# Exps of two attention layers turned in 32x32 blocks by VectorE, and their product in 16 or 8 blocks of TensorE's array

## The chip, the cores and the metric

The kernel runs on one core of a Trainium2 chip. A core has five engines, each of which works through its own instructions in the order in which they were put there: TensorE (PE in the profile, with its weight loads as PEld) multiplies matrices and writes to PSUM alone; VectorE (DVE), ScalarE (ACT) and GpSimd (POOL) work element by element; SyncE (SP) issues the DMAs. They wait for one another through semaphores. SBUF and PSUM have 128 partitions[...]. The metric is the device time of one execution in microseconds (us); lower is better. The kernel before takes 5228.07 us, the median of three runs (5227.61 to 5230.24).

## The reference

Four residual layers run over 32 independent graphs of 512 nodes with 256 features. Each layer norms its input, applies a ReLU, runs a graph attention under the graph's adjacency matrix, and adds the result to its input. Layers 0 and 3 are the ones that matter here; both are attention by dot products. Cut to that:

```python
# layer 0: H = 8 heads of HD = 32, queries = keys = values
qkv = layer_norm(x, gamma1, beta1).reshape(b_, n_, H, HD).transpose(0, 2, 1, 3)
scores = jnp.einsum('bhqd,bhkd->bhqk', qkv, qkv) * scale
masked = jnp.where(adj_matrix[:, None, :, :] > 0, scores, -jnp.inf)
attn = jax.nn.softmax(masked, axis=-1)
out = jnp.einsum('bhqk,bhkd->bhqd', attn, qkv)
x = x + out.transpose(0, 2, 1, 3).reshape(b_, n_, d_)
y = layer_norm(x, gamma2, beta2)
return x + jax.nn.gelu(y @ W1 + b1, approximate=False) @ W2 + b2

# layer 3: HEADS = 4 of D_K = 64, with projections q, k, v
scores = jnp.einsum('bnhd,bmhd->bhnm', q, k) * scale
attn = jax.nn.softmax(jnp.where(mask, scores, min_val), axis=-1)
out = jnp.einsum('bhnm,bmhd->bnhd', attn, v).reshape(B, N, OUT_DIM)
return jax.nn.relu(out @ Wo + bo)
```

Layers 1 and 2 are graph attentions whose logits are a sum of a term of the query and a term of the key (4 heads of 64). They are not changed. All is float32.

## The kernel before

**Tiling.** One graph ("batch" b) is held as 4 chunks of 128 rows (`NC = 4`, `P = 128`, `N = 512`, `D = 256`). `batch` (from L1726) strings the layers of one graph together: `layer0`, `gat_layer` twice, `layer3`.

**Order.** The program does not run in the order in which it is written. Every piece of work is an `Op` with an engine (or two that could do it), a planned cost in us, the tiles that it reads and writes, and the buffers that it needs. `Plan.schedule` plays all of them through with these planned costs and writes each engine's instructions down in the order in which they would start; up to `FLIGHT = 4` graphs are in flight, in `CHAINS = 3` chains. Which op goes first among those that could start is set by `key`, in which the constants `PACE`, `RAMP`, `SWITCH`, `URGENCY` and `FINE` enter. So the order is fixed at build time; on the chip an engine waits when what it needs is late.

**Attention of layers 0 and 3** (`attend`, `unit`). Heads go in groups of `G = P // dh`: four heads of 32 in layer 0, two of 64 in layer 3, two groups in each layer. For each half of the queries (two chunks of 128), each group and each query chunk:
- `dots` (L1078): scores of the G heads, each head in its own rows of the array (K = dh), 512 keys at once, into PSUM tiles `pss` of two banks (two buffers of those);
- for each head a `unit`: `masked` on DVE (L1125) scales the scores, adds the mask and takes the row's smallest value `low`, into SBUF tile `e`; `exps` on ACT (L1137) takes the exponential and its row sum; `turn` on PE (L1143) transposes the 128x512 exps in four transposes of 128x128 into PSUM bank `pst`; `evacuate` (L963) copies that bank to `eT` in SBUF, on DVE or ACT, whichever the plan picks.

After the two query chunks of a half, `product` (L1099) multiplies the values with `eT`: for each of the four key chunks and each head one matmul of 128 keys x dh values against 256 queries, each head in its own columns of the array, summed in bank `pso`. Then `finish`: layer 0 copies `pso` to `oT`, turns it back and divides by the row sums (`divide`, L1165 to L1182), and GpSimd adds it to `h` (L1502, L1503). Layer 3 spreads the reciprocals of the sums (L1649), turns them (L1656), multiplies them into `pso` (L1671), and projects (L1686 to L1693).

In float32 a matmul of the program that is no transpose stands as two matmul instructions in the trace, each with its own weight load; a transpose stands as one.

**Buffers.** Big tiles of 8 KiB per partition come from `exp_tile` (six buffers, tag "E"): two for a half of a group in layer 0, one in layer 3, two for a pair of heads in layers 1 and 2, two for the MLP's `gT`. The exps `e` of units have eight buffers of 2 KiB (`E_UNITS`). PSUM holds two tiles of two banks (`two`) and four of one bank (`one`).

**SP's queue.** SP issues the loads of the adjacency rows (L1715, two buffers, freed when POOL has made the mask of them at L1720), of x, and the stores.

```python
def turn(e):
    for c in ALL:
        nc.tensor.transpose(ps.t[:, c, :], ex.t[:, bass.ts(c, P)], ident)
```

## Time and profile before

The profiled execution took 5227.27 us, of which 5225.5 us are the span of the program's instructions; the granted clock of TensorE was 0.991 of full speed.

| what | value |
| --- | --- |
| median of three runs | 5228.07 us |
| profiled execution, its span | 5227.27 us, 5225.5 us |
| PE busy, share of the span | 97% |
| DVE, ACT, POOL busy | 61%, 70%, 52% |
| HBM traffic | 87.97 MB read, 16.78 MB written |

In a line of a group of instructions stand the line of the code, the engine, the operation, the tiles written and read with their shapes, the count after x, then busy time in us and the mean of one in ns, then the idle time of the engine before them and what ended it. Matmuls overlap in the array, so the mean of one matmul is longer than the step from one to the next. A busy time counts overlapping instructions once.

### The profile page before, as it was taken

To read this page: it belongs to the slowest core of one execution; us is meant where nothing else is said; L and a number is where in the kernel's file an instruction comes from. 1 tells how busy PE (TensorE), PEld (TensorE's weight loads), DVE (VectorE), ACT (ScalarE), POOL (GpSimd) and SP (SyncE) were. 2 spreads that over 40 slices of the span, in tenths; PEclk is the share of its full clock that TensorE was granted. 3 is DMA by queue.
4 is the path that set the end of the run, shared out by engine and by line. 5 is a ranking of instruction groups with operands and counts; after the bars stand their busy time and mean duration, and the time that the engine had idled before them with its cause. 6 is when DMAs were issued, how large, how long until landed. Compare 5 with 4: busy or idle time off the path is not lost.

```text
span 5225.5 us, 86599 instructions
## 1 busy us (share of the span) xinstructions
PE 5085.6 (97%) x30972; PEld 2810.8 (54%) x30972; DVE 3163.1 (61%) x9219; ACT 3668.6 (70%) x7053; POOL 2709.7 (52%) x3988
## 2 busy tenths in 40 slices
PE   6989999999999999999999999999999999999998
PEld 4544555555555555555555555555555555555554
DVE  5545666666565666565666666665656665666653
ACT  6747777777677777677776667776777766677755
POOL 6445544565544655445655445654446554456442
PEclk9989999999999999999999999999999999999999
DMA  2000000000000000000000000000000000000000
GB/s 84 1 9 25 20 10 21 25 25 25 17 11 23 25 25 25 11 15 25 25 25 19 11 21 25 25 25 15 13 23 25 25 25 15 11 25 25 13 13 13
DMA packets 78692, 110.31 MB, mean 21 GB/s; under 512 B 9523, under 2 KB 45238, under 8 KB 78262
## 3 DMA queue, kind: packets, MB, share of 16 engines
q1 hardware_dynamic: 70656, 100.68, 6.4%
q8 instruction: 246, 4.03, 0.3%
q10 hardware_dynamic: 7606, 4.08, 0.3%
q14 instruction: 184, 1.51, 0.1%
HBM read 87.97 MB, written 16.78 MB: 20 GB/s over the span
## 4 chain that ended last, share of the span: by engine, by line
PE 76%; POOL 13%; DVE 5%; ACT 3%; issue 2%; DMA 0%; ACTq 0%; POOLq 0%; SPq 0%; DVEq 0%
PE pst L1143 12%; PE pss L1078 9%; PE psg L1549 8%; PE psf L1528 8%; PE pso L1099 8%; POOL esum L1371 6%; PE psv L1574 4%; PE pso L1385 4%; PE psu L1441 3%; POOL mask L1720 2%; PE psk L1597 2%; PE psv L1625 2%; DVE junk L1260 2%; PE psq L1597 2%; PE psu L1433 2%
## 5 line engine op out<-in xcount | busy, mean ns | idle before, releaser
L1137 ACT ACTIVATE e<-e,low 128x512 f32<-128x512 f32 x1536 | 1102.5, 724 | 143.8 <-DVE low L1125 136.5
L1125 DVE CUSTOM_DVE_ANT_0 e<-pss,mask 128x512 f32<-128x512 f32 x1536 | 985.3, 682 | 253.3 <-PE pss L1078 212.8
L1143 PE MATMUL pst<-ident,e 128*128 128x128 f32 x6144 | 854.1, 278 | 29.9 <-ACT eT L963 20.2
L1143 PEld LDWEIGHTS pst<-ident,e 128*128 128x128 f32 x6144 | 673.0, 141 | 370.2 <-ACT e L1137 193.3
L1260 DVE CUSTOM_DVE_ANT_0 junk<-psd,mask 128x512 bf16<-128x512 f32 x1024 | 702.5, 686 | 124.3 <-PE psd L1248 93.8
L1371 POOL TENSOR_TENSOR esum<-esum,e 128x1024 f32<-128x1024 f32 x256 | 602.2, 2359 | 51.6 <-ACT e L1467 42.2
L1446 ACT ACTIVATE psu<-psu 128x1024 f32<-128x1024 f32 x512 | 509.1, 1011 | 164.7 <-PE psu L1441 164.0
L963 ACT COPY eT<-pst 128x512 f32<-128x512 f32 x954 | 520.7, 590 | 113.6 <-PE pst L1143 110.7
L1467 ACT ACTIVATE e<-psu 128x1024 f32<-128x1024 f32 x512 | 513.9, 1025 | 34.7 <-PE psu L1450 32.4
L1720 POOL TENSOR_SCALAR mask<-adj_mask 128x512 bf16<-128x512 int32 x256 | 494.2, 1931 | 53.8 <-DVE low L1125 19.1
L983 POOL TENSOR_TENSOR mw_h<-st_h 128x4 f32<-128x4 f32 x128 | 26.1, 204 | 935.4 <-DVE st_h L974 934.1
L1385 PE MATMUL pso<-e,hT 128*64 128x512 f32 x2048 | 474.8, 606 | 0.0
L1528 PE MATMUL psf<-yT,w_L_gnn_W 128*128 128x512 f32 x1024 | 457.0, 596 | 0.8 <-ACT gT L1539 0.8
L1549 PE MATMUL psg<-w_L_gnn_W,gT 128*128 128x256 f32 x2048 | 448.3, 379 | 0.4 <-ACT gT L1539 0.4
L963 DVE COPY eT<-pst 128x512 f32<-128x512 f32 x582 | 386.1, 685 | 83.2 <-PE pst L1143 73.2
L1549 PEld LDWEIGHTS psg<-w_L_gnn_W,gT 128*128 128x128 f32 x2048 | 386.4, 190 | 53.5 <-ACT gT L1539 1.2
L1371 POOL TENSOR_TENSOR esum<-e 128x1024 f32<-128x1024 f32 x128 | 301.1, 2352 | 171.6 <-ACT e L1467 160.5
L1502 POOL TENSOR_TENSOR od<-od,b_L_gnn_gamma 128x256 f32<-128x256 f32 x128 | 93.4, 730 | 519.9 <-DVE od L1182 519.7
L1008 ACT ACTIVATE h<-x,mv_h 128x256 f32<-128x256 f32 x512 | 272.2, 594 | 74.8 <-POOL mv_h L994 41.8
L1441 PE MATMUL psu<-maskT,ident 128*128 128x512 bf16 x1024 | 316.2, 391 | 0.0
L1539 ACT ACTIVATE gT<-psf,c_L_gnn_b 128x512 f32<-128x512 f32 x256 | 175.3, 689 | 196.4 <-PE psf L1528 195.9
L1528 PEld LDWEIGHTS psf<-yT,w_L_gnn_W 128*128 128x128 f32 x1024 | 188.0, 190 | 227.9 <-issue 204.5
(192 smaller groups left out, 8355.7 us busy)
## 6 DMA issues: line engine op xcount, KB each, us to landing
adj_mask<-in_adj SPq DMA_DIRECT2D x256, 256.0 KB, 2.6
x<-in_x SPq DMA_DIRECT2D x32, 512.0 KB, 3.9
out<-x SPq DMA_DIRECT2D x32, 512.0 KB, 3.2
w_L_gnn_W<-in_L_gnn_W ACTq DMA_DIRECT2D x2, 1024.0 KB, 6.6
w_L_gnn_W<-in_L_gnn_W ACTq DMA_DIRECT2D x1, 256.0 KB, 7.2
w_L_gnn_W_proj<-in_L_gnn_W_proj ACTq DMA_DIRECT2D x1, 256.0 KB, 7.4
w_L_gnn_Wo<-in_L_gnn_Wo ACTq DMA_DIRECT2D x1, 256.0 KB, 7.7
w_L_gnn_Wq<-in_L_gnn_Wq ACTq DMA_DIRECT2D x1, 256.0 KB, 7.1
```

Of the source, the lines that this page charges most:

```text
L963: lambda e: (nc.scalar.copy if e == "ACT" else nc.vector.tensor_copy)(dst(), view(src.t)),
L1125: nc.vector.tensor_tensor_reduce(out=ex.t, in0=src.t[:, j, :], in1=mask.t[:, q, :], scale=-scale, scalar=FLT_MAX, op0=ALU.add, op1=ALU.min ...
L1137: nc.scalar.activation(ex.t, ex.t, AF.Exp, bias=low.t, scale=-1.0, accum_out=total.t[:, q, h : h + 1])
L1143: nc.tensor.transpose(ps.t[:, c, :], ex.t[:, bass.ts(c, P)], ident)
L1260: nc.vector.tensor_tensor_reduce(out=junk.t, in0=dB.t, in1=mask.t[:, q, :], scale=1.0, scalar=-FLT_MAX, op0=ALU.add, op1=ALU.max, accum_ou ...
L1371: nc.gpsimd.tensor_tensor(esum.t, left, es[c // 2].t[:, c % 2, :, :], ALU.add)
L1385: nc.tensor.matmul(o.t[bass.ts(j, GD), :], v.t[:, c, bass.ts(2 * p + j, GD)], es[c // 2].t[:, c % 2, j, :], start=(c == 0), stop=(c == NC ...
L1446: nc.scalar.activation(ps.t, ps.t, AF.Prelu, alpha=SLOPE)
L1467: lambda e: nc.scalar.activation(dst.t[:, c % 2, :, :], ps.t, AF.Exp),
L1528: nc.tensor.matmul(ps.t, w1[:, d, bass.ts(f, P)], yT.t[:, d, :], start=(d == 0), stop=(d == DC - 1),)
L1549: nc.tensor.matmul(ps.t, gT[f // (FC // 2)].t[:, f % (FC // 2), bass.ts(c, P)], w2[:, f, :], start=(f == 0), stop=(f == FC - 1),)
L1720: lambda e, at=at, c=c: nc.gpsimd.tensor_scalar(mask.t[:, c, :], at.t, 0, -BIG, op, ALU.mult),
```

## The change

`unit` no longer turns the exps on PE, and nothing evacuates them. After `exps`, VectorE turns them in place in SBUF: `nc.vector.transpose` turns each 32x32 block of the 128x512 tile, but leaves the blocks where they are. So partition 32r + i, column 32k + b holds query 32r + b and key 32k + i of that chunk.

`product` therefore takes blocks of 32 keys. The array is used in pieces of 32 rows (32 keys; r, the block row of the queries) by dh columns (head j): 4 x 4 = 16 pieces in layer 0, 4 x 2 = 8 in layer 3. For each of 16 blocks k of keys, each r and each head one matmul: 32 keys x dh values against 128 queries (4 chunks of 32), summed over k in a PSUM bank of its own for each r. All four query chunks of a group go into one product, so there are two products for a layer of a graph in place of four.

Block row r needs the values of all keys on its partitions 32r to 32r + 31. `spread` makes this copy `vr` from the values in SBUF by 16 DMAs from SP for each group. The PSUM banks' columns come out in the order r, chunk, b, and `by_blocks` puts them back when they are copied or multiplied, in three parts (`parts_of`): two banks at once, then one and one.

A group takes G tiles of "E" for the exps of all chunks (`eT`) and one for `vr`, from eight buffers in place of six; the small tiles `e` are gone. Layer 3's reciprocals are spread and turned for the whole group ahead of the product (`prepare`). The plan's constants are set anew (of `URGENCY` and `FINE` nothing is shown).

```diff
-PACE = 24.3
-RAMP = 466.5
+PACE = 0.0
+RAMP = 393.0
-SWITCH = 150.8
-SKEW = {"DVE": 0.07, "ACT": 0.0}
-E_UNITS = 8
+SWITCH = 315.4
+SKEW = {"DVE": 0.12, "ACT": 0.0}
...
     def exp_tile(shape, name, b):
-        return Buf(att, shape, F32, "E", 6, name)
+        return Buf(att, shape, F32, "E", 8, name)
...
+        for g in range(H // G):
+            eT = [exp_tile([P, NC, N], f"eT_{name}_{g}_{j}", b) for j in range(G)]
+            vr = exp_tile([P, N // BL, P], f"vr_{name}_{g}", b)
+
+            def spread(e, g=g, vr=vr):
+                for r in range(P // BL):
+                    for m in range(P // BL):
+                        nc.sync.dma_start(
+                            vr.t[bass.ts(r, BL), m : N // BL : P // BL, :],
+                            v.t[bass.ts(m, BL), :, bass.ts(g, P)],
+                        )
+
+            plan.op(("SP", 9.0), spread, b, r=vkeys, w=[vr[0]], alloc=[vr, *eT])
+            for q in ALL:
...
+                plan.op(
+                    ("PE", 1.04), dots, b, r=qkeys(g) + kkeys(g),
+                    w=[t[i] for t in tiles for i in range(2)], alloc=[*tiles, vr, *eT],
+                )
+                for i in range(G):
+                    unit(eT[i], tiles[i // 2], i % 2, q, g * G + i, scale, mask, total, first, name, b)
+                    first = []
+            oT = result_tile(f"oT_{name}_{g}")
+            ready = prepare(g, oT, total)
+            o = [two(f"pso_{name}_{g}"), *(one(f"pso_{name}_{g}_{r}", [P, P]) for r in (2, 3))]
+
+            def product(e, g=g, eT=eT, vr=vr, o=o):
+                banks = [o[0].t[:, 0, 0:P], o[0].t[:, 1, 0:P], o[1].t, o[2].t]
+                for k in range(N // BL):
+                    for r in range(P // BL):
                         for j in range(G):
                             nc.tensor.matmul(
-                                o.t[bass.ts(j, dh), :],
-                                v.t[:, c, bass.ts(g * G + j, dh)],
-                                eT[j // 2].t[:, j % 2, c, :],
-                                start=(c == 0),
-                                stop=(c == NC - 1),
+                                banks[r][bass.ts(j, dh), :],
+                                vr.t[bass.ts(r, BL), k, bass.ts(j, dh)],
+                                eT[j].t[bass.ts(r, BL), :, bass.ts(k, BL)],
+                                start=(k == 0),
+                                stop=(k == N // BL - 1),
                             )
...
+            plan.op(
+                ("PE", 4.2), product, b, r=[vr[0], *ready, *(t[q] for t in eT for q in ALL)],
+                w=[t[0] for t in o], alloc=[*o, oT],
+            )
+            finish(g, o, oT, total)
...
         plan.op(
-            ("PE", 0.5), turn, b, r=[ex[0]], w=[ps[0]],
-            alloc=[ps, dst],
-        )
-        evacuate(
-            lambda: dst.t[:, j, :, bass.ts(qs, P)], [dst[j, qs]], ps, nm, b, N
+            ("DVE", 0.63), lambda e: nc.vector.transpose(ex.t[:, q, :], ex.t[:, q, :]), b,
+            w=[ex[q]],
         )
...
+        if isinstance(o, list):
+            for t, rs, view in parts_of(o):
+                cols = (rs.stop - rs.start) * P
+                plan.op(
+                    {"DVE": 0.07 + cols / 960, "ACT": 0.07 + cols / 1220},
+                    lambda e, rs=rs, view=view: (
+                        nc.scalar.copy if e == "ACT" else nc.vector.tensor_copy
+                    )(by_blocks(oT.t)[:, rs], view()),
+                    b, r=[t[0]], w=[oT[rs.start]],
+                )
```

## The prediction

> **What bounds the kernel now.** I read the page's busy line and chain first, then who waits for whom, then the groups by shape, then the timeline of one product, then DMA.
>
> ```profile
> PE 5085.6 (97%) x30972; PEld 2810.8 (54%) x30972; DVE 3163.1 (61%) x9219; ACT 3668.6 (70%) x7053; POOL 2709.7 (52%) x3988
> PE 76%; POOL 13%; DVE 5%; ACT 3%; issue 2%; DMA 0%; ACTq 0%; POOLq 0%; SPq 0%; DVEq 0%
> ```
>
> TensorE is the bound, all along the span: it waits for others for about 140 us in all. The waits list has its two largest here, the time in which matmuls (PE) and weight loads (PEld) sat idle for another engine; the second is mostly covered by matmuls that still run:
>
> ```profile
> PE pst L1143 <- ACT eT L963: 20.2, 31, 1.8
> PEld pst L1143 <- ACT e L1137: 193.3, 318, 1.6
> ```
>
> So what leaves PE's queue leaves the span, until another engine is late. The groups by shape that the change removes or multiplies:
>
> ```profile
> L1143 PE MATMUL pst<-ident,e 128*128 128x128 f32 x6144 | 854.1, 278 | 29.9 <-ACT eT L963 20.2 <-ACT e L1137 6.9 <-DVE qT L1608 0.6
> L1099 PE MATMUL pso<-eT,n 128*32 128x256 f32 x4096 | 249.7, 383 | 3.4 <-ACT eT L963 3.3
> L1099 PE MATMUL pso<-eT,hT 128*64 128x256 f32 x2048 | 249.3, 385 | 0.1
> ...
> L1125 DVE CUSTOM_DVE_ANT_0 e<-pss,mask 128x512 f32<-128x512 f32 x1536 | 985.3, 682 | 253.3 <-PE pss L1078 212.8 <-PE pst L1143 31.0 <-ACT e L1137 8.0
> L963 DVE COPY eT<-pst 128x512 f32<-128x512 f32 x582 | 386.1, 685 | 83.2 <-PE pst L1143 73.2
> L1125 DVE DVE_READ_ACCUMULATOR2_ANT low<- 128x1 f32 x1536 | 126.5, 82 | 0.0
> ...
> L963 ACT COPY eT<-pst 128x512 f32<-128x512 f32 x954 | 520.7, 590 | 113.6 <-PE pst L1143 110.7
> ```
>
> A product of layer 0 in the timeline (start and length in us): 32 matmuls of 256 columns in 1.93 us, although one takes 0.38.
>
> ```profile
> 4944.15 1.93 PE L1099 MATMUL pso<-eT,n 128*32 128x256 f32 x32
> ```
>
> In the trace's single starts it begins at 0, 6, 13 and 20 ns, then at 241, 246, 253, 260, and so on each 216 ns: four column pieces at a time, a next piece started 6.5 ns after the last, its weight load included. 216 ns for 256 columns are 0.84 ns a column. The two matmuls of one product stand next to each other in the instructions, yet the first of all four pieces start before any second: the queue looks ahead over at least 14 instructions.
>
> [...]
>
> **PE, part by part.**
> - Removed: 6144 transposes. Back to back one takes 109 ns (12 in 1.31 us), 670 us in all; with the drains around them the starts give 128 ns each, 786 us (the row's 854 us count the tails of the last ones too).
> - Removed: 128 + 128 products. From their first start to the next operation's start, 242 + 241 = 482 us.
> - Added: 64 products in layer 0 of 16 x 4 x 4 = 256 matmuls of the program, 512 instructions with 512 weight loads, and 64 in layer 3 with half as many. If all pieces run at once, each of 32 steps takes 128 columns x 0.84 = 108 ns: 3.5 us, with filling and drain 3.7 us for either layer, 128 x 3.7 = 474 us. In a step 16 starts x 6.5 ns = 104 ns just fit.
> - Sum: -786 - 482 + 474 = -794 us. The dots don't change.
>
> The unknown is the step with 16 pieces. Bounds: 6.8 ns a pair of load and matmul (above), or 27 ns (110 ns / 4) if no more than the four pieces shown ever run together. I take 6.8[...]. The instructions must also be fetched: the page's q8 moved 4.03 MB in 246 packets, 16 KB for 128 pairs, at about 1 us each (0.3% of 16 x 5225 us, over 246), which is 7.8 ns a pair: a product fetched no faster than that would take 4.0 us, within the range below.
>
> **DVE.** A block transpose of 128x512: [...]the nearest row, the copy of the same size, has 0.685. I take 0.70, 1536 x 0.70 = +1075 us. Low end 0.43 (the one SBUF copy of that size in float32, L875)[...]. Copies removed: -386. The list of instructions of the changed kernel also moves evacuations from DVE to ACT (hT, oT, qT, 245 us with their rows' means) and adds some: DVE comes to 3163 - 386 + 1075 - 227 = 3625 us.
>
> **ACT.** -521 for eT, +171 for what comes over from DVE, +128 for table loads (179 in place of 79, at 1283 ns): 3668 to about 3446 us. POOL's residuals halve in number and double in width: 2 x 0.73 against 1.27, -24 us.
>
> **SP and DMA.** 128 spreads x 16 = 2048 DMAs of 64 KB, each 128 rows of 512 B.
>
> ```profile
> q1 hardware_dynamic: 70656, 100.68, 6.4%
> q8 instruction: 246, 4.03, 0.3%
> q10 hardware_dynamic: 7606, 4.08, 0.3%
> ...
> SPq L1715 <- POOL mask L1720: 4347.0, 202, 202.6
> ```
>
> The first three are packets, MB and share of 16 engines; q10's packets, 536 B on average, took 33 ns, q1's of 1425 B took 76. So a spread takes 2048 x 33 / 16 = 4.2 us, at most 9.7, and SP issues it in 16 x 0.33 (one issue in the timeline) = 5.3 us. The cover is the group's units on DVE, (0.682 + 0.082 + 0.70) = 1.46 us each: 23 us in layer 0, 11.7 us in layer 3, where it is thin. Behind a spread in SP's queue stand the adjacency loads, which feed masks of later graphs. In front of it may stand a load that waits for POOL; the last line above shows that SP waits so nearly always, and a spread caught behind it would hold its product. I cost it at nothing, 2 us x 128 = 256 us at worst.
>
> **What is late next.** A group's units now need 1.46 us of DVE each where PE needs (297 + 280) / 1536 for the dots (rows of L1078) + 474 / 1536 = 0.68 us: attention alone is DVE-bound, and PE must fill in with other graphs. DVE in all would be 3625 of some 4500 us, 81% in place of 61%. The order is frozen from planned costs: 0.63 + 0.63 on DVE for a unit, against 1.46 measured or estimated, 0.2 us more. On 1536 units that is 307 us; before, DVE's idle 39% absorbed such errors. I let half through, +155 us. A layer 0 group holds five of eight E buffers, where two halves held two each of six; two groups of layer 0 can't overlap. That goes into the same 155.
>
> 5225.5 - 794 + 155 = 4586 us, and 1.8 us outside the span (5227.27 - 5225.5) make 4588. The median, 5228.07, lies 0.8 us above the profiled execution: 4589.
>
> **The rivals.**
> - *Part of it comes back* (17%): DVE becomes the bound in the attention stretches, the transposes cost 1 us or more, the E buffers keep graphs from overlapping, or the spreads come late. For: DVE at 81% with an order made for less. Against: PE, at 5085 - 794 = 4290 us, keeps 3240 us of other work to put beside these 1050. Time: DVE's 3625 us at 75% of the span, 4830 us; with transposes of 1 us, 3625 + 461 = 4086 us at 80%, 5110.
> - *The array or its queue doesn't run more than four pieces at once* (18%): the slower side. 64 x 512 + 64 x 256 = 49152 pairs decide: -786 - 482 is made up at 1268 us / 49152 = 25.8 ns a pair. At 27.5 ns the products take 1352 us: 5228 + 84 = about 5310 before any DVE stall; if only two run together (55 ns), 6660. For: nothing in the trace shows more than four pieces, or more than 14 instructions of look-ahead; no 3 us of it hold over 45 matmuls. Against: the evenness of 6.5 ns[...].
> - *Nothing to see* (3%): the two cancel, near 5230.
>
> **How the numbers follow.** The forecast, 62%, has its own range, 4400 to 4850: from -794 with no stall (4434) less a DVE transpose at the low end, to the full 307 us with half of the spreads late. To hold eight in ten the range takes in the first rival too, and ends where the second begins: 4360 to 5240. A change under 0.2% (10 us) could not be told from none. Faster: 62 + 17 - 1 = 78%; within 0.2%: 3%; slower: 19%.
>
> **What would show it.** Right: no pst at L1143's place, DVE transposes at 0.65 to 0.75 us, 512 matmuls of a product in 3.5 to 4.2 us, PE busy near 4300 us and still over 90%, DVE near 3600. Wrong: products over 7 us or in steps of four starts (second rival), PE idle before products, released by DVE's eT (first rival) or by the vr DMA (spreads).

## The result: slower by 18.6%, and the profile after

The changed kernel takes 6202.28 us, median of 4 runs (6191.45 to 6214.1), against 5227.84 us (4 runs, 5225.81 to 5230.24) for the kernel before, measured beside it: 1.1864 times as long, 95% interval 1.1841 to 1.1887. The forecast was 4589 us with a range of 4360 to 5240; the change is slower, and by far more than the slower rival priced for its likelier case (5310).

The page of the changed kernel, first its busy times and its chain of waits, then the granted clock of TensorE in 40 slices (tenths of full speed) and the instruction fetches:

```profile
PE 5351.7 (86%) x67706; PEld 2883.8 (46%) x67836; DVE 3550.6 (57%) x9669; ACT 3479.0 (56%) x6511; POOL 2687.0 (43%) x3860
PEclk7777888888888888888888888888888889888897
q8 instruction: 531, 8.70, 0.6%
PE 63%; ACT 15%; DVE 10%; issue 7%; POOL 2%; SPq 2%; DMA 1%; ACTq 0%; DVEq 0%; POOLq 0%
```

PE fell from 97% to 86% of the span, and other engines took its share of the chain: ACT 15% (3%), DVE 10% (5%), issue 7% (2%). VectorE and ScalarE are no fuller than before. The clock, 0.991 on average before, is 0.849; 1877 us of the span lie at half clock, 92 before. The 531 packets of q8, of 16 KB each, would at 256 instructions a packet be 135936, about the count of PE's weight loads and matmuls together (135542), so q8 carries PE's instructions. The clock before, and the dots of layer 0 before, for comparison:

```profile
PEclk9989999999999999999999999999999999999999
L1078 PE MATMUL pss<-qT 32*128 32x512 f32 x2048 | 297.4, 641 | 1.4 <-DVE low L1125 0.8
```

The groups by shape after:

```profile
L1118 PE MATMUL pso<-eT,vr 32*32 32x128 f32 x32768 | 670.4, 376 | 226.2 <-issue 185.4 <-DVE eT L1180 26.3 <-ACT e L1501 9.7
L1094 PE MATMUL pss<-qT 32*128 32x512 f32 x2048 | 474.7, 842 | 50.1 <-ACT e L1501 25.8 <-DVE low L1155 23.8 <-ACT qT L1058 0.3
L1118 PE MATMUL pso<-eT,vr 32*64 32x128 f32 x16384 | 290.9, 280 | 91.3 <-issue 70.8 <-DVE eT L1180 13.3 <-DMA vr<-hT 4.6
...
L1180 DVE STREAM_TRANSPOSE eT<-eT 128x512 f32<-128x512 f32 x1536 | 1005.5, 687 | 303.3 <-ACT eT L1167 302.8
```

The transposes of PE are gone, and VectorE's turn costs 687 ns. But the products stand at the top, with idle time that nothing the profile shows accounts for ("issue"), and the dots, whose program is unchanged, have grown from 297 to 475 us of busy time in layer 0. The waits of the changed kernel (us in total, times, longest):

```profile
ACT oT L1195 <- PE pso L1118: 659.9, 64, 15.9
DVE oT L1195 <- PE pso L1118: 551.5, 36, 19.4
ACT eT L1167 <- DVE low L1155: 540.7, 353, 9.3
...
DVE eT L1180 <- ACT eT L1167: 302.8, 131, 4.6
...
PE pso L1118 <- issue: 256.2, 235, 2.2
...
POOL mask L1757 <- DMA adj_mask<-in_adj: 227.8, 24, 35.1
...
PEld pss L1094 <- DVE low L1155: 201.4, 148, 4.4
```

VectorE and ScalarE stand waiting for products, up to 19 us at a time; and outside the products they wait for each other, and PE for VectorE. From the trace's single starts, each matmul counted up to the start of the next (so a wait behind a matmul counts with it), PE's time is:

| us | before | forecast | after |
|---|---|---|---|
| transposes | 786 | 0 | 0 |
| products | 482 | 474 | 1235 (853 + 382) |
| everything else | 3952 | 3952 + 155 | 4964 |

So the products alone take back nearly all that was removed (1235 of 1268), and everything else takes 1012 us more, which is the whole difference. As a yardstick take, for each shape, the median step from start to start at full clock before; a step counts as work up to that median. By it the 4964 divide into 2692 of work (2716 before), 264 of extra time in half-clock stretches (23) and 1998 of waits and drains (1204), with 10 us at the start left out of the sum. This yardstick puts too little down to the clock: where starts come in groups, a few ns apart and then a long step, the median is the short step, and what half clock adds to the long one lands in the waits. Compared instead with the step at the same place in the same run of matmuls before, the steps inside such runs that lie mostly at half clock took 397 us more (23 before). So the clock has well over a third of the 1012 us.

A product of layer 0 in the timeline (start, length, count, idle before it):

```profile
1807.32 3.01 PE L1118 MATMUL pso<-eT,vr 32*32 32x128 f32 x206 [0.18 <-DVE low L1155]
1811.79 2.35 PE L1118 MATMUL pso<-eT,vr 32*32 32x128 f32 x128 [1.46 <-issue]
1815.26 2.81 PE L1118 MATMUL pso<-eT,vr 32*32 32x128 f32 x128 [1.12 <-issue]
1818.73 1.40 PE L1118 MATMUL pso<-eT,vr 32*32 32x128 f32 x50 [0.66 <-issue]
```

It takes 12.7 us, not 3.7, and stops every 128 matmuls, which with their weight loads are 256 instructions, one block of 16 KB in q8. A block comes each 3.47 us here. Of the 266 gaps over 260 ns inside products some 250 stand at the same place modulo 256 instructions.

### The profile page after: what moved, and what is told of

Its sections match the earlier page's. It is cut to its first block, busy times and chain, and to the rows that moved or that the text cites. A ratio compares the mean times of both kernels' runs of the same rounds, so it can differ in the third digit from the quotient of the medians.

```text
span 6203.5 us, 161560 instructions
## 1 busy us (share of the span) xinstructions
PE 5351.7 (86%) x67706; PEld 2883.8 (46%) x67836; DVE 3550.6 (57%) x9669; ACT 3479.0 (56%) x6511; POOL 2687.0 (43%) x3860
## 4 chain that ended last, share of the span: by engine, by line
PE 63%; ACT 15%; DVE 10%; issue 7%; POOL 2%; SPq 2%; DMA 1%; ACTq 0%; DVEq 0%; POOLq 0%
PE pso L1118 14%; PE pso L1419 9%; PE pss L1094 8%; PE psg L1584 7%; DVE eT L1155 4%; PE psv L1609 4%; ACT eT L1167 3%; ACT e L1501 3%; PE psu L1475 3%; ACT psu L1480 2%; PE ps_hT L1042 2%; DVE eT L1180 2%; PE psq L1632 2%; ACT gT L1574 2%; PE psw L1722 2%
## 5 line engine op out<-in xcount | busy, mean ns | idle before, releaser
L1167 ACT ACTIVATE eT<-eT,low 128x512 f32<-128x512 f32 x1536 | 1095.1, 714 | 544.8 <-DVE low L1155 540.7
L1118 PE MATMUL pso<-eT,vr 32*32 32x128 f32 (+1 forms) x49152 | 961.2, 344 | 317.5 <-issue 256.2
L1180 DVE STREAM_TRANSPOSE eT<-eT 128x512 f32<-128x512 f32 x1536 | 1005.5, 687 | 303.3 <-ACT eT L1167 302.8
L1155 DVE CUSTOM_DVE_ANT_0 eT<-pss,mask 128x512 f32<-128x512 f32 x1536 | 985.9, 680 | 293.7 <-PE pss L1094 284.6
L1118 PEld LDWEIGHTS pso<-eT,vr 32*32 32x32 f32 (+1 forms) x49152 | 773.0, 129 | 523.0 <-issue 362.3
L1419 PE MATMUL pso<-e,hT 128*64 128x512 f32 x2048 | 584.9, 724 | 0.0
L1533 POOL TENSOR_TENSOR od<-od,b_L_gnn_gamma 128x512 f32<-128x512 f32 x64 | 81.5, 1273 | 1056.5 <-DVE od L1216 1056.5
L1094 PE MATMUL pss<-qT 32*128 32x512 f32 x2048 | 474.7, 842 | 50.1 <-ACT e L1501 25.8
L1456 POOL TENSOR_TENSOR x<-x,od 128x512 f32<-128x512 f32 x128 | 161.8, 1265 | 608.1 <-DVE od L1216 607.6
L1419 PEld LDWEIGHTS pso<-e,hT 128*64 128x64 f32 x2048 | 164.2, 169 | 439.1 <-issue 430.5
L1094 PE MATMUL pss<-kT,qT 64*128 64x512 f32 x1024 | 288.9, 653 | 89.8 <-DVE low L1155 89.3
```

The source lines that it names most:

```text
L1094: nc.tensor.matmul(tiles[i // 2].t[:, i % 2, :], qT.t[r0 : r0 + dh, g, bass.ts(q, P)], kT.t[r0 : r0 + dh, g, :], start=True, stop=True,)
L1118: nc.tensor.matmul(banks[r][bass.ts(j, dh), :], vr.t[bass.ts(r, BL), k, bass.ts(j, dh)], eT[j].t[bass.ts(r, BL), :, bass.ts(k, BL)], start ...
L1155: nc.vector.tensor_tensor_reduce(out=ex.t[:, q, :], in0=src.t[:, j, :], in1=mask.t[:, q, :], scale=-scale, scalar=FLT_MAX, op0=ALU.add, op ...
L1167: nc.scalar.activation(ex.t[:, q, :], ex.t[:, q, :], AF.Exp, bias=low.t, scale=-1.0, accum_out=total.t[:, q, h : h + 1],)
L1180: ("DVE", 0.63), lambda e: nc.vector.transpose(ex.t[:, q, :], ex.t[:, q, :]), b,
L1419: nc.tensor.matmul(o.t[bass.ts(j, GD), :], v.t[:, c, bass.ts(2 * p + j, GD)], es[c // 2].t[:, c % 2, j, :], start=(c == 0), stop=(c == NC ...
```

## The experiments

Three questions: what sets the time of a product, what makes everything else 1012 us longer, and whether a better kernel follows. "Outside" is PE's time outside the products (and, in kernels that have them, outside the transposes of exps), by matmul starts as above. The kernels are the changed one with the edit shown, unless said otherwise; the order of the work stays that of the changed kernel unless the planner's costs are touched. A time without an interval is that of a single execution.

### What sets the time of a product: e1 to e4, e10

**e1_narrow** halves the columns of the matmuls:

```
+ qs = slice(0, NC if k == 0 else NC // 2)
- eT[j].t[bass.ts(r, BL), :, bass.ts(k, BL)]
+ eT[j].t[bass.ts(r, BL), qs, bass.ts(k, BL)]
```

> The changed kernel with every product matmul after the first of each tile moving 64 columns where it moved 128: the same number of weight loads and matmuls in the same order, about half of the array's work (half of the queries are left out of all but the first block of the sum). Theory D (the products wait for the delivery of their instructions): a layer-0 product stays at 13.3 us (13.0 to 13.6), a layer-3 product at 5.5 to 5.9, the span within 1.5% of 6203. Rival A (the blocks themselves take the array's time, fewer than sixteen at once): layer-0 products fall to some 7 to 8 us, layer 3's to some 3.5, and the span by 400 us or more, to 5800 or less.

6248.99 us. Products 815 us in layer 0 and 375 in layer 3, 12.7 and 5.9 us each, against 13.3 and 6.0: half of the array's work is gone and nothing is gained. The group of layer 0:

```profile
L1119 PE MATMUL pso<-eT,vr 32*32 32x64 f32 x30720 | 478.4, 293 | 312.8 <-issue 312.8
```

The busy time fell, the idle time for "issue" rose. By gap between starts in layer 0 (us, after and e1): up to 12 ns 92 and 146; 12 to 60 ns 324 and 194; 60 to 260 ns 157 and 89; over 260 ns 258 and 371, in 195 and 196 gaps. The stalls stay as many and get longer by what the steps between them get shorter: what comes at a fixed pace is the block of instructions. The clock does not set this pace either: inside the products of the changed kernel the transfers of q8 start 3.53 us apart at half clock (median of 83) and 3.62 us elsewhere (86), in e1 3.52 and 3.73. Rival A falls.

**e2_half** sums over half of the keys:

```
- for k in range(N // BL):
+ for k in range(N // BL // 2):
```

> The changed kernel with the second half of each product's sum left out (8 of the 16 blocks of keys): half of its instructions, each as wide as before. Theory D: layer-0 products at 5.5 to 6.5 us, layer 3's at 2 to 2.7 (the first 32 to 40 pairs of a product leave a filled queue at 7 ns each, and those weigh more), so 1235 us of products become 480 to 590; the time at half clock, which follows the long sparse products, falls by more than half from 1877 us, and other PE work takes 250 to 400 us less: a span of 5100 to 5350. Rival B (order, fewer exp buffers and the longer DVE chain keep the other PE work slow; the products cost only their own time): the span falls by no more than the 650 to 750 us of the products, to 5450 to 5550.

5692.86 us. Products 373 + 264 = 637 us (5.8 and 4.1 us each; layer 3's look above what was expected, but 103 of their 264 us lie behind the last matmul, where PE already waits for its next work; from first to last start they take 2.5 us each, as expected). The time fell by 509 us for 598 us of products, less than either theory said; outside rose to 5049 us, and half clock fell only to 1543.

**e4_single** reads the operands as bfloat16, so that a matmul is one pass (16384 in layer 0 and 8192 in layer 3 in the trace, 32768 and 16384 in the changed kernel):

```
- vr.t[bass.ts(r, BL), k, bass.ts(j, dh)]
+ vr.t.bitcast(BF16)[bass.ts(r, BL), k, 2 * j * dh + 1 : 2 * (j + 1) * dh : 2]
```

and the same for eT.

> The changed kernel with the product's operands read as bfloat16 (the upper half of each float32 word, so the products are less exact): a matmul is then one pass, and a product issues half of the instructions, 256 pairs in layer 0 and 128 in layer 3; order, waits and all other work as they were. Theory D: layer-0 products 5 to 6.5 us, layer 3's 1.8 to 2.7, time at half clock less than half of 1877 us, span 5000 to 5350, so about the time of before or a little under. Rival A: with one pass for two the array's time halves as well, so this run does not tell A from D (the narrow one does). Rival B: no more than the 650 to 750 us of the products, 5450 to 5550.

5693.01 us, 1.089 times before (1.0871 to 1.0908). Products 312 + 246 = 557 us, 4.9 us in layer 0, below the expected range, and 3.8 in layer 3, above it; but 125 of layer 3's 246 us again lie behind the last matmul, and from first to last start its products take 1.9 us each, in the range. Without the waits behind them all products take 417 us. This is about the 474 us of the forecast or less, and the kernel is still 1104 us over it. Half clock stays at 1748 us, outside is 5126. So the products' price explains 509 us of the change from 5228 to 6202, and something else the rest.

**e3_dense** puts full 128x128 matmuls in the products' place (124 in layer 0, 52 in layer 3):

```
+ nc.tensor.matmul(banks[r], vr.t[:, i % (N // BL), :],
+     eT[i % G].t[:, i % NC, bass.ts(r, P)], ...)
```

> The changed kernel with each product replaced by full 128x128 matmuls of 128 columns that fill about the same time (124 in layer 0, 52 in layer 3; the attention outputs are then meaningless numbers): the same place in the order, the same waits. Theory D: the product's time stays 13 to 15 us and 5.5 to 6.5, but the array is full in it: time at half clock falls from 1877 us to under 400, PE work outside the products takes 400 to 700 us less, and the span is 5500 to 5800. Rival B (the clock falls because PE stands waiting for VectorE and ScalarE, whatever the product is): time at half clock stays above 1000 us (outside the products about the 1200 that it is now) and the span above 6000.

7527.74 us. I had sized the filler wrongly: the two passes of such a matmul take 118 ns each (2658 us over 22528), so a filler lasts 30 us, not 13. What can be read: the time at half clock fell from 1877 to 1238 us, by 413 us inside the products (681 to 268) and only 227 outside (1196 to 970), and outside fell by 101 us to 4863. The products' emptiness is a small part of the loss outside; theory D's larger claim, that it is most of it, falls.

**e10_rows** turns the loops:

```
- for k in range(N // BL):
-     for r in range(P // BL):
+ for r in range(P // BL):
+     for k in range(N // BL):
```

> The changed kernel with the product's loops turned round: the block of rows outermost, so that only the 4 (layer 0) or 2 (layer 3) pieces of one block of rows can run at once, and not 16 or 8; the same instructions, operands and banks. A single piece streams 128 columns and its neighbours' waits are those of 4 or 2 at once: by the old product's 16 pieces of 256 columns in 1.88 us each piece of 128 has about 27 ns of array for itself with four at once, 54 with two. Theory D (delivery at 16 ns a pair with stalls, 26 ns on average in layer 0, is the limit there and the packing beyond four is unused): layer-0 products stay at 13 to 14.8 us; layer 3's rise from 5.7 to 12 to 14.5, since two at once are slower than the delivery; span 6500 to 6800. If sixteen at once is what layer 0's time rests on (theory A), its products rise to 25 us or more and the span to 7200 or more.

7976.28 us; layer 0's products 23.9 us, layer 3's 21.3. Both above what theory D gave, and layer 0's nearly at A's figure. But the clock is the reason:

```profile
PEclk7676677777777777777777777777777777777776
L1118 PE MATMUL pso<-eT,vr 32*32 32x128 f32 x32768 | 1531.6, 402 | 40.3 <-DVE eT L1180 26.3 <-ACT e L1501 9.8 <-DVE low L1155 2.6
```

2533 of the products' 2892 us are at half clock. A pair takes 26.5 ns in layer 0 at full clock and 48.0 at half, in layer 3 54.5 and 95.9: the 27 and 54 ns of the expectation hold where the clock is full. There are no "issue" waits left in the row: now the array is slower than the delivery. So more than four pieces do run at once in the changed kernel's order, whose layer 0 products take 26 ns a pair although they lie mostly at half clock (646 of 853 us). And products that use a quarter of the rows at a time ran at half clock nearly throughout.

### What makes everything else longer: e5 to e9, e11, e13 to e15, e17

**e5_turn32** takes most of VectorE's turn away:

```
- nc.vector.transpose(ex.t[:, q, :], ex.t[:, q, :])
+ nc.vector.transpose(ex.t[:, q, 0:BL], ex.t[:, q, 0:BL])
```

> The changed kernel with VectorE turning only the first 32 of each unit's 512 columns (the other 480 stay as they are and go into the product unturned); everything else as it was, products included. Theory V (the time outside the products, 4964 us, rose because each exp now passes VectorE twice, with ScalarE between, and PE waits for it): VectorE's busy time falls by some 850 to 950 us from 3551, PE's waits in the dots fall by half, and the span falls by 350 us or more, below 5850. Theory C (it rose because the array lost the work that held its clock: 1877 us at half speed) and theory P (the order) say little change: the span stays within 150 us of 6203, the time at half clock above 1500 us.

6169.51 us. VectorE's rows:

```profile
L1155 DVE CUSTOM_DVE_ANT_0 eT<-pss,mask 128x512 f32<-128x512 f32 x1536 | 991.9, 684 | 447.3 <-PE pss L1094 446.7
L1180 DVE STREAM_TRANSPOSE eT<-eT 128x32 f32<-128x32 f32 x1536 | 270.5, 195 | 530.6 <-ACT eT L1167 521.3
```

735 us of VectorE's work are gone, and its waits for ScalarE's exps grew from 303 to 521 us, those for the dots from 285 to 447. The span kept all but 33 us. Theory V falls, for this order.

**e6_warm** adds array work ahead of the dots:

```
+ for t in tiles:
+     nc.tensor.matmul(t.t[:, 0, :], qT.t[:, g, bass.ts(q, P)], kT.t[:, g, :],
+                      start=True, stop=True)
```

> The changed kernel with full 128x128 matmuls of 512 columns put ahead of the dots, one for each two heads (768 in all, overwritten by the dots; at full clock about 0.43 us each, 328 us together): the array gets back part of the dense work that the transposes were. Theory C: the time at half clock falls from 1877 us to under 900, the clock loss in the work outside the products (264 us by the durations) to under 120, and the span stays at 6200 or falls to 6000 although 328 us were added. Theory V: the fillers lie in PE's waits for VectorE, so the span rises by less than 150 us, but it doesn't fall, even with the clock back. If neither holds (PE has no room and the clock isn't held by it), the span rises by the whole 328 us or more, to 6500.

6708.66 us, 506 more. The filler was twice what I had sized: each stands as two matmuls of 0.43 us, 1536 in the trace, 659 us by the yardstick and not 328. The granted clock rose from 0.849 to 0.882, and half clock fell to 1585 us only. The clock's extra time outside (264 us by the first yardstick) became 312, but 137 of it is that of the fillers themselves; in the rest it fell to 175. So dense work gave part of the clock back, at a higher price; as a remedy theory C has nothing to show, and as a part of the cause it is not cleared.

**e7_costs** gives the planner the durations of the trace:

```
- ("PE", 4.2), product        + ("PE", 13.3 if G == 4 else 6.0), product
- ("DVE", 0.63), masked       + ("DVE", 0.78), masked
- ("ACT", 0.72), exps         + ("ACT", 0.92), exps
- ("DVE", 0.63), turn         + ("DVE", 0.70), turn
```

> The changed kernel with the costs that its trace shows given to the planner: product 13.3 us in layer 0 and 6.0 in layer 3 (4.2), masked 0.78 (0.63), exps 0.92 (0.72), turn 0.70 (0.63); the same operations in another order. Theory P (the order was laid out for a product of 4.2 us and lighter units, so VectorE and ScalarE run dry in the products and PE waits after them): the span falls by 300 us or more, to 5900 or less, with the products themselves still at 13.3 and 5.5 to 6 us. Theories C and V: within 150 us of 6203.

7198.36 us, with the same operations and with products of 1283 us: outside went to 5909, half clock to 3121 us. Better costs gave a far worse order, because the priorities beside them were fitted to the old costs. That outside moves by 945 us with the order alone says where to look.

**e11_order** is e7 with URGENCY, FINE, PACE, RAMP, SWITCH and SKEW searched anew, by small random changes kept when the planner's own schedule gets shorter:

```
- PACE = 0.0           + PACE = 42.3
- RAMP = 393.0         + RAMP = 1658.3
- SWITCH = 315.4       + SWITCH = 3694.6
```

and so on through both tables.

> The changed kernel with the planner told the durations of its own trace (product 13.3 and 6.0 us, masked 0.78, exps 0.92, turn 0.70) and its priorities searched anew for these, where the earlier run changed the durations alone: the same operations, buffers and banks in another order. Theory P (the time outside the products is what the order leaves, and an order laid for a product of 4.2 us leaves too much): outside 4500 to 4750 us instead of 4964, span 5750 to 6050. If the buffers and the chains between the engines keep it there whatever the order, outside 4900 or more and the span within 150 us of 6203.

6096.72 us; products 1273, outside 4817, between the two cases. An order laid for the true durations is better by 106 us; that the plan had products of 4.2 us costs about that, by what this search found.

**e8_mixed** is the kernel before with layer 3 alone changed, its new operations given the priorities of those they replace, product entered at 6.0:

```
- attend(H, dh, v, values(v), qT, lambda g, half: [qT[g, half]], ...)
+ attend3(H, dh, v, values(v), qT, lambda g: qT.parts((g, 0), (g, 1)), ...)
+ "3:unit3.exps:eT": -287.1,
```

with attend3 and unit3 the changed kernel's attend and unit.

> The kernel before with layer 3 alone in the changed form (layer 0 keeps its transposes, its halves of queries and its product; 6 exp buffers as before; layer 3's product entered at 6.0 us). Theory D prices it so: 2048 transposes (262 us) and layer 3's old products (about 240 us) go, 64 products of 5.5 to 6 us (350 to 385) come: -120 to -150 on PE, against the loss of array work in layer 3's stretches. If the time outside grows only where layer 0's transposes went (theory C mostly there): 5080 to 5230. If each unit that moves to VectorE costs what the whole change showed, 1010 us for 1536 units, 0.66 us a unit: +337 us for 512 units, 5400 to 5500.

6088.83 us, 1.1636 times before (1.1617 to 1.1655). Far above both figures. Layer 3's products took 441 us, layer 0's transposes and products, which are as they were, 576 + 246. After e7 the reading is that a patched order costs hundreds of us whatever it holds; the run says nothing sure of layer 3.

**e9_few** leaves almost nothing of the products:

```
- for k in range(N // BL):
+ for k in range(1):
```

> The changed kernel with 15 of the 16 blocks of keys left out of every product: 32 load-and-matmul pairs stay in layer 0, 16 in layer 3, all from a filled queue, so 0.2 to 0.4 us a product and under 60 us for all 128; order and waits as they were. If the products alone had spoilt the result, PE's other work would now stand as densely as the forecast had it, and the span would be 4100 to 4400 us. If the time outside the products is a cost of its own that no product length changes (4964 us in the changed kernel, 5049 with half a product, 5126 with single passes), the span is 4980 to 5200, hardly below the 5228 of before although 1268 us of matmul work are gone from PE.

5629.51 us. The products' rows, and the page's busy line:

```profile
L1118 PE MATMUL pso<-eT,vr 32*32 32x128 f32 x2048 | 49.4, 351 | 41.4 <-DVE eT L1180 27.4 <-ACT e L1501 9.8 <-DVE low L1155 2.6
L1118 PE MATMUL pso<-eT,vr 32*64 32x128 f32 x1024 | 47.5, 309 | 20.0 <-DVE eT L1180 13.1 <-DMA vr<-hT 6.9
```

```profile
PE 4628.5 (82%) x21627; PEld 2191.0 (39%) x21756; DVE 3545.9 (63%) x9669; ACT 3474.7 (62%) x6511; POOL 2685.6 (48%) x3860
```

Of 1268 us of transposes and products 258 are left, 180 of which are waits behind the last matmul of a product, and the kernel is 400 us slower than before. Outside alone is 5365 us, above the 4980 to 5200 that I had expected of the whole span: in this order outside grew as the products were shortened (4964 us beside products of 1235 in the changed kernel, 5049 beside 637 in e2, 5126 beside 557 in e4). No engine but PE is over 63%.

**e13_few_turn32** joins the edits of e9 and e5.

> The changed kernel with both cuts in one: 15 of the 16 blocks of keys left out of the products, and VectorE turning 32 of each unit's 512 columns. Some 900 us of VectorE's 3546 and 1200 us of PE's products are then gone. If VectorE's second pass is what binds once the products are short, the span falls from 5628 to 5100 or less. If the wait is spread over the chain PE, VectorE, ScalarE, VectorE, PE of an order that stays the same, each cut gives a part only: 5400 to 5520. No change (5580 or more) would clear VectorE altogether.

5591.53 us, 38 less than e9: the last of the three cases. In this order VectorE's work is not what binds, even with the products away.

**e15_adj_pool** moves the mask loads off the queue of the spreads:

```
- nc.sync.dma_start(at.t, adj[b, bass.ts(c, P), :])
+ nc.gpsimd.dma_start(at.t, adj[b, bass.ts(c, P), :])
```

> The changed kernel with the loads of the adjacency rows issued by GpSimd, which reads them, and no longer by SP, where the spreads stand ahead of them and wait for exp buffers (GpSimd waited 228 us for these loads in 24 places; before, not in its list). If the masks' lateness is a good part of the time outside the products, the span falls by 100 us or more, to 6100 or less; if it is hidden like the spreads themselves, it stays within 60 us of 6203.

6191.45 us. GpSimd's waits for these loads halved, from 228 to 114 us (11.5 in the kernel before), and the span stayed.

**e14_few_order** was to be e9 in an order searched for it, but the cut was missing from its kernel, so it ran whole products of 13.3 and 6 us in an order laid for products of 0.4 and 0.3:

```
- ("PE", 4.2), product
+ ("PE", 0.4 if G == 4 else 0.3), product
```

with the unit costs of e7.

> The changed kernel with 15 of the 16 blocks of keys left out of the products, the planner told so (0.4 and 0.3 us) and given the measured costs of the units, and its priorities searched anew. If the order laid for other durations is what holds the 5628 us of the same cut in the old order, this falls to 5000 or below. If the scheme itself (longer chains, one group of exps of layer 0 in the buffers at a time, banks held by the product) leaves the waits in any order: 5200 to 5400, so that the change could hardly have won even with products that cost nothing.

6449.2 us, products 1245, outside 5197. It tells only that an order laid for short products is worse for long ones (e11: 6096.72). **e17_few_order** is the same order with the cut.

> The changed kernel with 15 of the 16 blocks of keys left out of every product, in the order of e14, searched anew for products of 0.4 and 0.3 us and the measured costs of the units. If the old order, laid for other durations, is what holds the 5628 us of the same cut: 5000 or below. If the scheme itself leaves the waits in any order that the search finds: 5200 to 5400.

5322.55 us, in the range of the scheme: 307 us under e9 by order alone, still 93 us over the kernel before. What PE's products wait for now, and the row of matmuls that waits longest:

```profile
L1115 PE MATMUL pso<-eT,vr 32*32 32x128 f32 x2048 | 63.2, 347 | 128.1 <-DVE eT L1177 116.4 <-ACT e L1498 11.6
L1606 PE MATMUL psv<-waug,hT 128*128 128x264 f32 x1024 | 346.1, 497 | 185.6 <-ACT hT L962 185.6
```

The first wait is for VectorE's turns, so in this order VectorE is not cleared; the second stands before the projections with which layers 1 and 2 begin, outside the changed attention. Outside is 5200 us: 2723 of work, 286 of clock, 2181 of waits and drains, by the first yardstick above; by the comparison with the same place before, the clock has 361 us. The products left, with the waits behind them, take 116 us. Taking these off as well would leave some 5206 us, an estimate, hardly below the 5229 of the kernel before. So in the order that the search found, products for next to nothing don't beat the transposes; whether they would at the clock of before is not shown.

### A version that is better: e12, e18, e16

**e12_single_order** is e4 with the planner told 4.9 and 3.8 us and the unit costs of e7, priorities searched anew.

> The kernel with single-pass products (operands read as bfloat16) with the planner told the durations of its trace (product 4.9 and 3.8 us, masked 0.78, exps 0.92, turn 0.70) and its priorities searched anew for them: the best version that these runs suggest. Theory P: products 500 to 580 us as they were, outside 4800 to 4950 instead of 5126, span 5350 to 5550. If the order isn't the cause: within 100 us of 5693. It beats the kernel before only if the outside falls below 4650.

5539.32 us, 1.059 times before (1.0572 to 1.0607), in the expected range: 154 us better than e4 by order, but with outside at 5027, above the expected 4800 to 4950. (The 3.8 us told to the planner for layer 3 held the waits behind the product; its products take 111 us in all here.)

**e18_half_before_old** takes the kernel before and lets its transposes and products read bfloat16, so that exps and values are less exact, in its own order:

```
- nc.tensor.transpose(ps.t[:, c, :], ex.t[:, bass.ts(c, P)], ident)
+ nc.tensor.transpose(ps.t[:, c, :], ex.t.bitcast(BF16)[:, 2*c*P + 1 : 2*(c+1)*P : 2], ident16)
```

with ps and the stored eT in bfloat16.

> The kernel before with the single-pass transposes and products of e16, but in its own old order. If the cheaper work on PE does it alone: 4900 to 5000. If an order laid for the dearer work gives back only part, as in the changed kernel: 5050 to 5180.

5211.16 us, 18 under the kernel before. Transposes fell from 786 to 616 us and products from 482 to 311, waits in and behind them included (211 of the 311 lie behind the last matmul), and everything else rose from 3952 to 4277. The row and the wait that took the place:

```profile
L1143 PE MATMUL pst<-ident,e 128*128 128x128 bf16 x6144 | 569.9, 229 | 212.2 <-ACT e L1137 161.3 <-ACT eT L963 29.3 <-DVE oT L963 4.2
```

Before, matmuls of this row waited 6.9 us for ScalarE's e; now 161.3. The order, not the work, holds this kernel's time. **e16_half_before** is the same with transposes of 0.3 us a unit and products of 1.0 entered and the priorities searched anew:

```
- ("PE", 0.5), turn      + ("PE", 0.3), turn
- ("PE", 1.95), product  + ("PE", 1.0), product
```

> The kernel before, not the changed one, with the single-pass idea of the earlier run: PE's transposes and the products of layers 0 and 3 read the upper half of each float32 exp and value as bfloat16, the turned exps are stored as bfloat16, and the priorities are searched anew for transposes of 0.3 us a unit and products of 1.0. PE is dense in this kernel (97%), so less work on it should come off nearly in full: 6144 transposes at 128 ns to some 70 to 80 (-300 to -350 us) and 256 products at 1.88 us to about 1.0 (-220), 4750 to 4950 us, faster than both. If PE then waits as it does in the changed kernel: 5050 to 5200.

4874.88 us, 0.9323 times before (0.9307 to 0.9338), faster than both kernels:

```profile
L1139 PE MATMUL pst<-ident,e 128*128 128x128 bf16 x6144 | 521.3, 221 | 38.0 <-ACT e L1133 25.5 <-DVE grt L1258 6.1 <-ACT eT L959 2.0
L1095 PE MATMUL pso<-eT,n 128*32 128x256 bf16 x2048 | 98.4, 278 | 2.3 <-ACT eT L959 2.0 <-DVE oT L959 0.2
```

```profile
PE 4629.0 (95%) x27900; PEld 2394.4 (49%) x27900; DVE 2994.6 (61%) x9200; ACT 3771.3 (77%) x7182; POOL 2699.3 (55%) x3988
```

The wait is down to 25.5 us and PE at 95%. Transposes take 524 us (85 ns each), products 172.

## Why the prediction was wrong, step by step

- **Removed, 786 + 482 us: right.** No transposes at that place, and the old products are gone.
- **Added products, 6.8 ns a pair, 3.7 us each, 474 us: wrong, 1235 us.** (6.8 ns is layer 0's price; over both layers the forecast's 474 us are 9.6 ns a pair.) The starts of 6.5 to 7 ns are met only in the first 32 to 40 pairs of a product, and there too only within a set of 8 or 16 pieces: with the waits between the sets these pairs take 13.7 ns on average in layer 0 at full clock and 19.7 at half. After them half of the steps in layer 0 lie between 13 and 20 ns, with a median of 16 to 17, and at the edges of the instruction blocks the starts stop. Of the two bounds the lower was chosen, an estimate from the even starts of the old product; the trace before showed no more than four pieces at once and 14 instructions of look-ahead. The average is 25.1 ns a pair (1235 us / 49152), close to the upper bound of 27 ns and to the break-even of 25.8, but for another reason: the pace of the instruction blocks, 3.5 us for 128 pairs. The array's four-piece limit, the second rival's mechanism, was not it (e10 at full clock reaches just those 27 and 54 ns and has no issue waits; e1 halves the array's work for nothing). The fetch was in the working, as 7.8 ns a pair and 4.0 us a product "within the range": that took the transfer of a 16 KB block, about 1 us, as its rate. The trace has one block each 3.47 us, and by the DMA records a stalled matmul mostly goes on 2.3 to 2.9 us after the last block transfer before it began, though that took 0.9 to 1.4. Why the next transfer starts no sooner stays open. Some 250 of the 384 block edges in the products cost 0.3 to 2.4 us each. The price of the term: 6202 - 5693 = 509 us, by e4, where the products cost 557.
- **"So what leaves PE's queue leaves the span", with 155 us for late orders: wrong by more than the first.** With products at 557 us the kernel takes 5693 (e4), at 258 us 5630 (e9), so the forecast would have failed with its product priced right. PE did not stay dense. The runs show what this is not: in the changed kernel's order, VectorE's turns (e5, e13), the product's length (e1, e2, e4, e9), the mask loads (e15). They show that the order is a good part of it: outside moves between 4817 and 5909 us by order alone (e11, e7), e17 gains 307 us over e9, and in the kernel before 341 us of PE's time taken away give 18 us in the old order (e18), and the same cut 355 us with an order searched for it (e16). The clock has another part (next point). What is left, 5322.55 us with products of next to nothing (e17), the search found no order for; how much of that is the scheme's own is not shown. The forecast charged the mis-planned units 155 us; the planned order as a limit of its own had no term.
- **The clock: missing.** By the first yardstick 264 us of the time outside the products are the cost of half clock, by the comparison with the same place before 397, against 23 before. The forecast took PE's other durations as fixed; the dots of layer 0, at 641 ns before, have a mean of 842. That less work on the array could go with a lower clock (0.991 before, 0.849 after) was not thought of.
- **VectorE's turn 0.70 us, 1075 in all, an estimate beside the copy's 0.685: right**, 0.687 and 1005.5; VectorE's total 3550.6 for 3625, ScalarE's 3479 for 3446 and GpSimd's 2687 for 2686 also. "VectorE is 81% full" is wrong only because the span is longer.
- **Spreads at nothing: right where it was priced.** Products waited 4.6 us for them in all. The adjacency loads behind them were late, as the working feared (228 us on GpSimd); e15 shows that this cost nothing.
- **The rivals.** The first named VectorE, the E buffers and the spreads; in the changed kernel's order VectorE (e5, e13) and the spreads (4.6 us of waits) are cleared, but in e17's order products do wait for VectorE's turns (116 us). The buffers were not tried, as two groups of layer 0 at once found no room. The second had the sign and the break-even right, and the place (products over 7 us), but gave 5310 us since it left the rest of PE alone.

Open: which part of the scheme keeps PE waiting in e17. The longer chain of a unit (PE, VectorE, ScalarE, VectorE, PE in place of PE, VectorE, ScalarE, PE), the single group of exps of layer 0 in its buffers, the four banks that a product holds, and the clock are each possible; none was tried alone in a re-laid order. The clock alone costs e17 some 340 us more than the kernel before, by the comparison above, which is more than the 93 us by which it is slower. And an order search finds a good order, not the best.

## What to carry to other kernels

Before pricing a stream of many small matmuls by its first starts, ask how many instructions it has: here, past its first 32 to 40 pairs, a product of layer 0 ran at the pace of its instruction blocks, 128 pairs in about 3.5 us, and half the instructions (a single pass, e4) took all products from 1235 to 557 us, where half the columns (e1) left 1190. And in a kernel whose order is laid out ahead, work taken from the busiest engine is worth what the next wait allows: e18 kept 18 us of 341 until the order was laid anew (e16). Test the upper bound of a change first, with the new operation cut to nothing in an order made for it; here that run alone (5322.55 us) would have said no.

## What the runs showed of the hardware

- **Small pieces do overlap, and beyond four.** In the changed kernel's trace, among the first pairs of layer 3's products at full clock, eight starts at 7 ns and 63 ns of wait make a step of 109 ns, as the forecast's 108 ns for all pieces at once. In layer 0 at half clock, sixteen starts of 6 to 11 ns and a wait of 103 ns make 221 ns, about twice 108. At full clock e10 has 26.5 ns a pair with four at once and 54.5 with two.
- **The stalls at instruction blocks** were not expected: in the changed kernel 195 gaps over 260 ns in layer 0, 258 us, and 71 in layer 3, 98 us, between 0.3 and 2.4 us each.
- **Half clock followed stretches in which the array did little.** The clock records in the traces of both kernels last multiples of 3.41 us. Cut into windows of that length, with the columns started in each times their share of the 128 rows as its load (as a unit for counting, 8192 columns of 128 rows in a window are 1), the kernel before went from full to half clock after all 8 windows under a load of 0.25 and after one of the 1482 above (at 0.40); the changed kernel after all 21 under 0.15, some 126 of 284 between 0.15 and 0.35, and some 43 of 948 above. So little work goes before half clock, but the load as counted here draws no sharp line. Dense work in the products' place took 413 us of half clock out of them (e3). Weighted by columns alone the windows separate less well (those of 0.6 to 0.7 went to half in 37%). That the rows count is argued from this, and from e10's products, which use 32 of them at a time; no run changed the rows alone.
